# First attention of a gated cross-attention kernel: normalized rows in transposed form, from an input that is laid out transposed as well

## The chip, the core and the metric

The kernel runs on one core of a Trainium2 chip. The core has engines that each take their own instructions in order: TensorE (PE in the profile, with its weight loads as PEld), VectorE (DVE), ScalarE (ACT), GpSimd (POOL) and SyncE (SP), which here issues most of the transfers; sixteen DMA engines move the data. [...] SBUF is the on-chip memory with 128 partitions, PSUM the small memory that PE writes to, DRAM the memory outside. The metric is the device time of one execution in microseconds (us); lower is better.

## What is computed

The reference is a block of two layers on x, two sequences of 2048 rows with 512 features:

```python
x = x + tanh(g_xattn[0]) * xattn0(layernorm(x), ctx)
x = x + tanh(g_ffn[0])   * ffn0(layernorm(x))      # router takes 256 rows of each sequence
x = x + tanh(g_xattn[1]) * xattn1(layernorm(x), ctx)
x = x + tanh(g_ffn[1])   * ffn1(layernorm(x))      # quantized, with a convolution
```

The change is in the first line. There, layernorm takes each row's own mean and variance over the 512 features, without learned factors:

```python
m = mean(x, axis=-1); v = var(x, axis=-1)
xn = (x - m) / sqrt(v + 1e-5)
q = xn @ Wq.T + bq          # 16 heads of 32
att = softmax(q k^T / sqrt(32))       # over the 128 rows of the context
out = (att v) @ Wo.T + bo
```

Keys and values come from the context alone and are made once, at the start. The queries are a product over the features, so PE wants the normalized rows with the features on the partitions: xn transposed.

## The kernel before

The 4096 rows are worked in N = 8 blocks of BLK = 512 rows (TB = 4 tiles of 128 rows; DC = 4 chunks of 128 features). A block has H = 16 units, one for each head. `cross_attention` is a function used for both attentions; in its main loop, U counts units over all blocks, n is the block and u the unit in it, and four units make a group with one query tile qT.

For each unit the loop asks for: scores on PE (once for four heads, into four PSUM tiles sc), the maxima of the scores on DVE (`nmx`, L119), four exponentials on ACT (L122), a reciprocal on DVE (L130) and the division on POOL (L131), all within `probabilities`; two units later, four transposes of the attention weights A on PE (`tp`, L297) and their copy AT by DVE or ACT (L298); after each four units, the product with the values on PE (`po`, L305) and a copy OT by ACT. After a block's last group, the generator `back` is advanced one step for each unit: POOL adds the output bias to the rows of x (L322), PE makes the output projection (`pp`, L328), DVE adds it to x (L339). Then the router of that block runs beside the next block's units: statistics of the new rows (L817), a dot product (L821), a store of x, a scaled row xo on ACT (L845) which is stored, the loads of x for three blocks on, and the ranking by comparisons (`marks` L873, `tie` L917).

What comes before a block's queries is `front(n)`. Before the change it is asked for at unit `ahead` = 10 of the block before: `ln_stats` takes bn_stats and their aggregate on DVE (L99, L100), a small step on DVE (L88) and a power on POOL (L90) for 1/sqrt; `normalize` makes four tiles xn on DVE (L104); `transpose_block` transposes them in sixteen steps on PE into PSUM tiles ptr (L113), and ACT copies those to xnT (L245). `queries` then multiplies xnT with Wq on PE (`pq`, L256), and ACT makes qT with scale and bias (L264). pq, ptr and pp share one PSUM pool, ps_mm, with two buffers. The first block's front stands alone, before the loop.

The order of instructions on each engine isn't the order of the source. A scheduler of the framework builds each engine's order from the requests, moving work forward where it finds an engine free and the buffers allow it; so the row statistics of blocks 1 and 2 stand ahead of the first block's first maxima, already before the change. Once built, the order is fixed, and each engine waits at the head of its own queue. SP's queue is one such order: a transfer that must wait holds those behind it.

At the start, SP loads the context and the key and value weights, four tiles of x, then Wq, biases, Wo, the router's weights, and eight more tiles of x.

Of the kernel before, what the change touches and what calls it, by code (L numbers as in the profile page):

```python
# [10 lines left out]
F32 = mybir.dt.float32  # L11
BF16 = mybir.dt.bfloat16
AF = mybir.ActivationFunctionType
ALU = mybir.AluOpType
# [29 lines left out]
def flamingo_kernel(ctx: ExitStack, tc: tile.TileContext, a: dict, out: bass.AP):  # L44
# [172 lines left out]

    def cross_attention(
        W, act, hold, ps_mm, ps_sc, ps_o, row, xnT_bufs, ahead, rows_of, after_block, beside,
        after_units=lambda: None,  # L220
    ):

# [11 lines left out]
        if bias:  # L234
            nc.vector.tensor_scalar(W.bq, W.bq, scale, None, ALU.mult)

        def front(n):

            tiles, xn, residual = rows_of(n)
            mv, rstd = ln_stats(tiles, L + "ln")  # L240
            for i, t in enumerate(tiles):
                normalize(xn[i], t, mv, rstd, i)
            xnT = act.tile([P, DC, BLK], F32, name="xnT", tag="xnT", bufs=xnT_bufs)
            transpose_block(
                ps_mm, "mm", xn, lambda d, pt: nc.scalar.copy(xnT[:, d, :], pt)  # L245
            )
            return residual, xnT

        def queries(xnT, grp):

# [95 lines left out]


        N = B * NBLK
        residual, xnT = {}, {}
        residual[0], xnT[0] = front(0)  # L350
        next_qT = queries(xnT[0], 0)
        As, AT, OT, out_of = {}, {}, {}, iter(())
        for U in range(N * H + 12):
            n, u = divmod(U, H)
            if n < N:
                grp, t = divmod(u, 4)
                if t == 0:
                    qT = next_qT
                if u % hpc == 0:
                    sc = scores(n // NBLK, qT, u // hpc)  # L360
                As[U] = probabilities(sc[u % hpc])
                if u == ahead and n + 1 < N:
                    residual[n + 1], xnT[n + 1] = front(n + 1)
                if t == 1 and grp < 3:
                    next_qT = queries(xnT[n], grp + 1)
                elif t == 1 and n + 1 < N:
                    next_qT = queries(xnT[n + 1], 0)
            V = U - 2
            if 0 <= V < N * H:
# [386 lines left out]
    with ExitStack() as st:  # L756
# [239 lines left out]

        sel_pools = selected_pools(st)
        W0 = CrossWeights("L0_", D // P, True, gx[0], st, "left")
        nc.scalar.dma_start(out=W0.bk, in_=a["L0_bk"])
        nc.scalar.dma_start(out=W0.bq, in_=a["L0_bq"])  # L1000
        with ExitStack() as st0:
            loads = W0.load_keys(st0, "left")
            next(loads)
            next(loads)
            load_x(0)
            for _ in loads:
                pass
# [22 lines left out]
        for q in selecting:  # L1030
            for _ in q:
# [450 lines left out]
def laid_out(i):  # L1482
# [6 lines left out]
    def col(v, n):  # L1489
# [53 lines left out]
```

## Time and profile before

| | us |
|---|---|
| median of 3 runs | 1741.56 (1740.54 to 1748.13) |
| the profiled execution | 1741.68, of which its span 1740.0 |
| PE busy | 1628.8 (94% of the span) |
| DVE busy | 1240.6 (71%) |
| ACT busy | 1103.3 (63%) |
| POOL busy | 560.1 (32%) |
| first queries of the first attention start | 27.3 |
| first row maxima (L119) start | 33.6 |
| last scores of the first attention start | 497.6 |
| granted clock of TensorE, mean share of full speed | 0.982 |

How to read it: the span is the time between the first and the last instruction of one profiled execution; the rest of its time lies around it. Busy is the sum of an engine's instruction times, in which those that overlap aren't counted twice. A group row of the profile gives the line, the engine, the operation, what it writes and reads with partitions x elements and type, how many there are, then the busy time, the mean of one in ns, and the time for which the engine stood idle just before them, with whom it waited for. A busy share over the whole span is a mean over stages with different limits. The first attention takes about the first 30% of it.

### The profile page before, as it was taken

The page shows a single profiled execution, that of the slowest core. Times are in us where ns is not written, and L with a number is a line of the kernel's source. Part 1 is how long each engine was busy: PE and PEld are TensorE (multiplying, and loading weights), DVE is VectorE, ACT ScalarE, POOL GpSimd, SP SyncE. Part 2 cuts the span into 40 slices and gives each one's busy share as a digit, 9 for nine tenths or more (in the row PEclk, how much of TensorE's full clock was granted, in tenths as well). Part 3 has the DMA queues.
Part 4 walks back from the last instruction along what each step waited for, and adds up shares of the span by engine and source line. Part 5 has one row for each costly group of instructions (what it writes and reads, how often), then busy time and mean ns, then how long its engine had stood idle before and what let it go on. Part 6 is the DMA issues. An engine that isn't in the chain of part 4 may idle for free.

```text
span 1740.0 us, 25223 instructions
## 1 busy us (share of the span) xinstructions
PE 1628.8 (94%) x8076; PEld 856.4 (49%) x8122; DVE 1240.6 (71%) x2576; ACT 1103.3 (63%) x3170; POOL 560.1 (32%) x703
## 2 busy tenths in 40 slices
PE   7999888899999989999999999999999999998988
PEld 4545444455555665755454544445444454444433
DVE  5566777865757543345368889898789889877986
ACT  2876566456553333345267878788787887855575
POOL 2534443442340021033223243343332333343221
PEclk9999999999989999999999999999999999999999
DMA  6011111121005851920011334234133233157294
GB/s 222 7 68 56 37 62 68 61 67 55 25 37 197 274 174 63 300 85 25 19 55 73 122 99 148 92 115 164 73 128 115 88 103 132 78 217 264 100 311 149
DMA packets 116973, 196.99 MB, mean 113 GB/s; under 512 B 13117, under 2 KB 51517, under 8 KB 113129
## 3 DMA queue, kind: packets, MB, share of 16 engines
q1 hardware_dynamic: 110664, 177.54, 29.5%
q0 software_dynamic: 5888, 17.83, 3.2%
q8 instruction: 64, 1.05, 0.2%
q14 instruction: 69, 0.56, 0.1%
q10 hardware_dynamic: 288, 0.00, 0.0%
HBM read 120.89 MB, written 74.45 MB: 112 GB/s over the span
## 4 chain that ended last, share of the span: by engine, by line
PE 48%; DVE 27%; ACT 9%; issue 6%; DMA 6%; POOL 3%; SPq 0%; DVEq 0%; POOLq 0%; ACTq 0%
PE pp L328 12%; PE pq L256 9%; DVE h L1196 4%; PE po L305 4%; PE tp L297 4%; PE sc L279 4%; ACT A L122 3%; PE ph L1179 3%; DVE nmx L119 2%; DVE marks L873 2%; DVE u L1190 2%; DVE AT L298 1%; DMA x<-h_d 1%; DVE L_ln_st L99 1%; DMA h_d<-h 1%
## 5 line engine op out<-in xcount | busy, mean ns | idle before, releaser
L122 ACT ACTIVATE A<-sc,nmx 128x128 f32<-128x128 f32 x1024 | 364.7, 386 | 122.6 <-DVE nmx L119 117.9
L131 POOL TENSOR_TENSOR A<-A,rden 128x512 f32<-128x512 f32 x256 | 280.5, 1098 | 493.9 <-DVE rden L130 402.4
L328 PE MATMUL pp<-L_wo,OT 128*128 128x512 f32 x768 | 360.8, 601 | 5.4 <-DVE x L339 5.4
L256 PE MATMUL pq<-xnT,L_wq 128*128 128x512 f32 x768 | 344.8, 596 | 1.3 <-DVE x L339 1.2
L122 ACT ACTIVATION_READ_ACCUMULATOR A<-sc,nmx 128x1 f32 x1024 | 229.5, 224 | 0.0
L256 PEld LDWEIGHTS pq<-xnT,L_wq 128*128 128x128 f32 x768 | 142.5, 191 | 159.7 <-issue 151.4
L119 DVE TENSOR_REDUCE nmx<-sc 128x4 f32<-128x512 f32 x256 | 168.7, 679 | 67.7 <-PE sc L279 67.6
L328 PEld LDWEIGHTS pp<-L_wo,OT 128*128 128x128 f32 x768 | 134.9, 191 | 148.9 <-issue 130.9
L1196 DVE SCALAR_TENSOR_TENSOR h<-u,cw,h 128x512 f32<-128x512 f32 x256 | 197.2, 803 | 5.8 <-ACT h L1192 5.3
L297 PE MATMUL tp<-ident,A 128*128 128x128 f32 x1024 | 164.8, 285 | 23.5 <-POOL A L131 12.4
L297 PEld LDWEIGHTS tp<-ident,A 128*128 128x128 f32 x1024 | 118.6, 143 | 93.2 <-issue 47.5
L298 DVE COPY AT<-tp 128x512 f32<-128x512 f32 x192 | 130.0, 679 | 38.7 <-PE tp L297 38.1
L279 PEld LDWEIGHTS sc<-L_kT,qT 32*128 32x128 f32 (+1 forms) x2048 | 109.7, 189 | 70.8 <-issue 58.2
L279 PE MATMUL sc<-L_kT,qT 32*128 32x128 f32 (+1 forms) x2048 | 136.2, 291 | 3.7 <-ACT A L122 3.1
L1192 ACT ACTIVATE h<-u,cb,cw 128x512 f32<-128x512 f32 x128 | 99.5, 809 | 62.1 <-DVE u L1190 57.1
L305 PE MATMUL po<-AT,L_v 128*32 128x512 f32 (+1 forms) x512 | 120.1, 655 | 11.5 <-DVE AT L298 11.1
L1409 PE MATMUL po<-w2q,hq 128*128 128x512 bf16 x501 | 117.6, 381 | 9.8 <-ACT hq L1389 6.2
L1179 PE MATMUL ph<-xiT,w1q 128*128 128x512 bf16 x477 | 122.5, 379 | 2.1 <-DVE u L1190 0.2
L1190 DVE TENSOR_TENSOR u<-ph,inv_b 128x512 f32<-128x512 f32 x128 | 85.4, 683 | 31.5 <-PE ph L1179 27.7
L130 DVE RECIPROCAL rden<-den 128x4 f32<-128x4 f32 x256 | 43.6, 170 | 80.3 <-ACT A L122 72.7
L1189 POOL COPY u<-carry 128x2 f32<-128x2 f32 x112 | 44.3, 397 | 150.3 <-DVE h L1196 127.7
L1179 PEld LDWEIGHTS <-w1q 128*128 128x128 bf16 x512 | 49.2, 98 | 79.1 <-issue 35.3
(246 smaller groups left out, 2383.1 us busy)
## 6 DMA issues: line engine op xcount, KB each, us to landing
h_d<-h SPq DMA_DIRECT2D x28, 1024.0 KB, 3.9
x_d<-x SPq DMA_DIRECT2D x64, 256.0 KB, 2.0
hf<-h_d SPq DMA_DIRECT2D x64, 256.0 KB, 3.0
x<-h_d SPq DMA_DIRECT2D x48, 256.0 KB, 5.3
x<-in_x SPq DMA_DIRECT2D x32, 256.0 KB, 3.7
x_d<-xo SPq DMA_DIRECT2D x32, 256.0 KB, 2.0
xf<-x_d SPq DMA_DIRECT2D x32, 256.0 KB, 3.5
x<-x_d SPq DMA_DIRECT2D x32, 256.0 KB, 3.4
```

What stands on the lines that cost most here:

```text
L119: nc.vector.tensor_reduce(nmx, sc, AX.X, ALU.max, negate=True)
L122: nc.scalar.activation(out_tile[:, h, :], sc[:, h, :], AF.Exp, bias=nmx[:, h : h + 1], accum_out=den[:, h : h + 1],)
L131: nc.gpsimd.tensor_tensor(out_tile, out_tile, rden.unsqueeze(2).to_broadcast([P, n, width]), ALU.mult,)
L256: nc.tensor.matmul(pq, W.wq[:, d, ts(e, P)], xnT[:, d, :], start=(d == 0), stop=(d == DC - 1),)
L279: nc.tensor.matmul(sc[h][:, t, :], qT[e % cpg][r, ts(t, P)], W.kT[r, b, e, :], start=True, stop=True,)
L297: nc.tensor.transpose(tp[:, t, :], A[:, t, :], ident)
L298: copy(AT, tp.rearrange("p t n -> p (t n)"))
L305: nc.tensor.matmul(po[h * dh : (h + 1) * dh, :], W.v[:, b, ts(hd, dh)], AT[c * hpc + h], start=True, stop=True,)
L328: nc.tensor.matmul(pp, OT[e][:, ts(i, P)], W.wo[:, e, :], start=(e == 0), stop=(e == nE - 1),)
L1179: nc.tensor.matmul(ph, w1q[:, d, ts(c, P)], xiT[g][:, d, :], start=(d == 0), stop=(d == DC - 1),)
L1190: nc.vector.tensor_tensor(u[:, 2:], ph, inv_b[g], ALU.mult)
L1196: nc.vector.scalar_tensor_tensor(z, u[:, ds(k, BLK)], cw[:, c, k : k + 1], z, ALU.mult, ALU.add)
```

## The change

The input x is given to the kernel a second time, transposed (`xT`, 512 features x 4096 rows). A block's normalized transposed rows are then made in that layout, as xT * (1/sqrt(v+eps)) + (-m/sqrt(v+eps)), where both factors run along the free dimension and must be the same in all 128 partitions. To spread them over the partitions, the first block uses eight PE transposes (`bcast_rows`) into two PSUM tiles; the others write the two 128 x 4 columns to DRAM as rows and load them back, 4 KB into each partition (SP issues all of it). The multiplication is done by DVE in the first block and by POOL in the others, the addition by DVE. The row statistics are still taken from x in its own layout, with DVE and POOL.

The second attention keeps the old way. `front` becomes a generator; one step of it is taken for each unit, from unit 5 of the block before. The first queries of the next block are asked for one unit later in the last group (t == 2 in place of t == 1). A pool xTp with two buffers of 1 MB holds xT; the tiles xn and xnT of this attention are gone, and a tile ln_sp of 4 KB per partition is new. xT of the first block is loaded behind the first four tiles of x.

```diff
     def cross_attention(
         W, act, hold, ps_mm, ps_sc, ps_o, row, xnT_bufs, ahead, rows_of, after_block, beside,
-        after_units=lambda: None,
+        after_units=lambda: None, columns_of=None,
     ):
...
         def front(n):
-            tiles, xn, residual = rows_of(n)
+            if columns_of:
+                residual[n], xnT[n] = yield from columns_of(n)
+                return
+            tiles, xn, residual[n] = rows_of(n)
...
-            return residual, xnT
+            yield
...
-        residual[0], xnT[0] = front(0)
+        for _ in front(0):
+            pass
+        rows_for = iter(())
+        starts = {max(0, n * H + ahead): n + 1 for n in range(N - 1)}
...
-                if u == ahead and n + 1 < N:
-                    residual[n + 1], xnT[n + 1] = front(n + 1)
+                if U in starts:
+                    rows_for = front(starts[U])
+                next(rows_for, None)
                 if t == 1 and grp < 3:
                     next_qT = queries(xnT[n], grp + 1)
-                elif t == 1 and n + 1 < N:
+                elif t == 2 and grp == 3 and n + 1 < N:
                     next_qT = queries(xnT[n + 1], 0)
...
+        xTp = st.enter_context(tc.tile_pool(name="xTp", bufs=2))
+        def load_xT(n):
+            t = xTp.tile([P, DC, BLK], F32, name="xT", tag="xT")
+            nc.sync.dma_start(out=t, in_=row_tiles(a["xT"])[:, :, ts(n, BLK)])
+            return t
...
             load_x(0)
+            xT0 = load_xT(0)
...
-        def stage1_rows(n):
+        def stage1_columns(n):
             tiles = [x[t] for t in range(n * TB, (n + 1) * TB)]
-            xn = [act.tile([P, D], F32, name="xn", tag="xn", bufs=TB) for _ in tiles]
-            return tiles, xn, lambda: tiles
+            xT = xT0 if n == 0 else load_xT(n)
+            st = small.tile([P, TB, 6], F32, name="L0_ln_st", tag="ln_st")
+            mv = small.tile([P, TB, 2], F32, name="L0_ln_mv", tag="ln_mv")
+            for i, t in enumerate(tiles):
+                nc.vector.bn_stats(st[:, i, :], t)
+                nc.vector.bn_aggr(mv[:, i, :], st[:, i, :])
+                if n > 0 and i == 1:
+                    yield
+            rstd = rsqrt(TB, mv[:, :, 1], 1.0, 1e-5, small, "L0_ln_rstd")
+            nmr = row.tile([P, TB], F32, name="nmr0", tag="nmr0")
+            nc.vector.scalar_tensor_tensor(nmr, mv[:, :, 0], -1.0, rstd, ALU.mult, ALU.mult)
+            if n == 0:
+                spread = [ps_mm.tile([P, BLK], F32, name="pb0", tag="mm") for _ in range(2)]
+                for ps, cols in zip(spread, (rstd, nmr)):
+                    bcast_rows(ps, cols, ident)
+            else:
+                sp_d = dramp.tile([2, TB, P], F32, name=f"ln_d{n}")
+                with nc.allow_non_contiguous_dma("columns to rows"):
+                    for k, cols in enumerate((rstd, nmr)):
+                        nc.sync.dma_start(out=sp_d[k].rearrange("j n -> n j"), in_=cols)
+                yield
+                sp = act.tile([P, 2, BLK], F32, name="ln_sp", tag="ln_sp", bufs=1)
+                nc.sync.dma_start(
+                    out=sp.rearrange("p k n -> p (k n)"),
+                    in_=sp_d.rearrange("k j n -> (k j n)").partition_broadcast(P),
+                )
+                spread = [sp[:, k, :] for k in range(2)]
+                for _ in range(3):
+                    yield
+            for d in range(DC):
+                to = xT[:, d, :]
+                scaler = nc.vector if n == 0 else nc.gpsimd
+                scaler.tensor_tensor(to, to, spread[0], ALU.mult)
+                nc.vector.tensor_tensor(to, to, spread[1], ALU.add)
+                if d % 2:
+                    yield
+            return lambda: tiles, xT
...
-            W0, act, act, ps_mm, ps_sc, ps_o, row, 1, 10, stage1_rows,
+            W0, act, act, ps_mm, ps_sc, ps_o, row, 1, 5, None,
             lambda n, tiles: pending.append(router(n, tiles)), beside,
+            columns_of=stage1_columns,
...
         "x": con(np.asarray(i["x"]).reshape(B * S, D)),
+        "xT": con(np.asarray(i["x"]).reshape(B * S, D).T),
```

In the order that is built from this, POOL's queue in the first block holds four divisions, the four multiplications of block 1, eight divisions, the four multiplications of block 2, and then the divisions from the thirteenth on.

More of the change, by code (lines that the diff above doesn't have):

```diff
@@ L235, in cross_attention @@
             nc.vector.tensor_scalar(W.bq, W.bq, scale, None, ALU.mult)
+        residual, xnT = {}, {}
         def front(n):
-            tiles, xn, residual = rows_of(n)
+            if columns_of:
+                residual[n], xnT[n] = yield from columns_of(n)
+                return
+            tiles, xn, residual[n] = rows_of(n)
             mv, rstd = ln_stats(tiles, L + "ln")
@@ L242, in front @@
                 normalize(xn[i], t, mv, rstd, i)
-            xnT = act.tile([P, DC, BLK], F32, name="xnT", tag="xnT", bufs=xnT_bufs)
+            xnT[n] = act.tile([P, DC, BLK], F32, name="xnT", tag="xnT", bufs=xnT_bufs)
             transpose_block(
-                ps_mm, "mm", xn, lambda d, pt: nc.scalar.copy(xnT[:, d, :], pt)
+                ps_mm, "mm", xn, lambda d, pt: nc.scalar.copy(xnT[n][:, d, :], pt)
             )
-            return residual, xnT
+            yield
         def queries(xnT, grp):
@@ L348, in cross_attention @@
         N = B * NBLK
-        residual, xnT = {}, {}
-        residual[0], xnT[0] = front(0)
+        for _ in front(0):
+            pass
+        rows_for = iter(())
+        starts = {max(0, n * H + ahead): n + 1 for n in range(N - 1)}
         next_qT = queries(xnT[0], 0)
```

## The prediction

> **What bounds the kernel now.** I read the 40 slices first, to find which engine is full where; then busy times per stretch of the first attention (about 32 to 525 us); then its groups by shape, for the price of each operation; then the waits and the chain, for what is late.
>
> The slices, engine and tenths busy:
>
> ```profile
> PE   7999888899999989999999999999999999998988
> DVE  5566777865757543345368889898789889877986
> POOL 2534443442340021033223243343332333343221
> ```
>
> A slice is 43.5 us, so the first twelve digits are this attention: TensorE (PE) at eight or nine tenths, VectorE (DVE) at five to eight, GpSimd (POOL) at two to five. By stretch (length, then busy time and instructions of PE, weight loads, DVE, ACT, POOL; clock, DMA share, GB/s):
>
> ```profile
> 33.00:90.00 57.00, 54.20 (x387) 30.09 (x382) 31.11 (x74) 47.15 (x217) 30.05 (x28) 1.00 0.02 6
> 90.00:150.00 60.00, 55.33 (x367) 28.98 (x364) 42.61 (x102) 40.38 (x169) 25.08 (x23) 1.00 0.17 58
> 205.00:265.00 60.00, 52.99 (x360) 27.58 (x353) 45.65 (x102) 37.41 (x154) 25.02 (x22) 1.00 0.16 54
> ```
>
> PE idles 2.8 us in the first stretch and 4.7 and 7.0 in the others; adding the windows between them gives 45.6 us over 33 to 525. So PE bounds, with holes where DVE is late: freed PE time is worth its full length only while nobody else arrives later. The groups that the change touches, in 32 to 525 us:
>
> ```profile
> L113 PE MATMUL ptr<-ident,xn 128*128 128x128 f32 x112 | 17.4, 279 | 0.6 <-ACT qT L264 0.5
> L245 ACT COPY xnT<-ptr 128x512 f32<-128x512 f32 x28 | 16.4, 596 | 15.2 <-PE ptr L113 9.9 <-PE pi L963 5.2
> L104 DVE TENSOR_SCALAR xn<-x,L_ln_mv,L_ln_rstd 128x512 f32<-128x512 f32 x24 | 15.7, 707 | 7.9 <-POOL L_ln_rstd L90 7.8
> L131 POOL TENSOR_TENSOR A<-A,rden 128x512 f32<-128x512 f32 x128 | 141.5, 1110 | 219.6 <-DVE rden L130 184.4 <-DVE m L547 9.6 <-PE pq L256 9.1
> L322 POOL TENSOR_TENSOR x<-x,L_bo 128x512 f32<-128x512 f32 x31 | 40.2, 1298 | 0.0
> ```
>
> The first three are what goes. The fourth is the softmax division that every attention weight passes; what I put on POOL ahead of it delays it. The fifth, two full SBUF inputs, is the nearest row for the new multiplications. Who is late for whom (total us, times, longest):
>
> ```profile
> ACT A L122 <- DVE nmx L119: 75.9, 27, 6.7
> PEld tp L297 <- POOL A L131: 25.8, 22, 2.7
> PE tp L297 <- POOL A L131: 10.6, 12, 2.2
> ```
>
> PE already waits for the division, and the exponentials wait for the row maxima, which stand in DVE's queue. At the start the chain is DVE alone (start, length, what):
>
> ```profile
> 21.36 0.70 DVE L_v L213
> ...
> 22.61 1.00 DVE xn L104 x2
> ...
> 30.03 1.92 DVE xn L104 x4
> ...
> 33.63 0.65 DVE nmx L119
> ```
>
> From 22.15 us to the first maximum at 33.6 DVE works almost without a gap: 11.5 us, nothing to hide in. The transfers nearest to the new ones (size, us to landing):
>
> ```profile
> x_d<-x SPq DMA_DIRECT2D x64, 256.0 KB, 2.0
> xf<-x_d SPq DMA_DIRECT2D x32, 256.0 KB, 3.5
> ```
>
> **The sum, against 1741.7 us** (span 1740.0 and 1.7 around it; the median of the runs is 0.1 lower). I use start-to-start distances: DVE 0.60 for a two-input 128x512 operation or a maximum, 0.80 for bn_stats with its aggregate, 0.48 for xn; PE 0.43 for four transposes; POOL 1.27 and 1.04 for the last two groups.
>
> *Removed.* Per block 16 transposes: 4 x 0.43 = 1.7 us of PE, which sits between other matmuls and so counts. Four ACT copies (4 x 0.6 = 2.4 us) and four xn are off the PE queue.
>
> *xn becomes add, four each.* The Trainium skill (VectorE: DVE Perf Modes, "Why tensor_tensor can't do 2x_2P or 4x") says that a two-tensor operation can't use the doubled f32 mode that a one-tensor operation from SBUF can. At 512 elements and its 0.96 GHz that would be 0.27 against 0.53 us, hence 1.1 us more per block (an estimate from the page). The rows give 0.48 and 0.60: 0.5 us more. And the mean of xn here is 0.71 where its median is 0.54 (one took 1.48 beside a POOL operation), so the old form was not at its best either. I take the rows: 0.5 us, on DVE, small beside what follows.
>
> *Start, +4.2.* The scale and shift rows are made by 8 PE transposes behind the last value matmul (21.3 + 0.9 = 22.3 us). Then DVE's order is: 4 multiplications, 4 additions and both value additions (one was done at 18.8 before): 10 x 0.60 = 6.0; bias gate and weight sum 1.0; bn_stats of the next two blocks 8 x 0.80 = 6.4; two eps steps and two shifts 0.66; waits for POOL's power (1.02 each, the second in full) 1.4. Together 15.5: the first maximum at 37.8, 4.2 later. Before, eight plain xn did this. PE has meanwhile only the second group's queries (3.5 us) and then waits for the first A. The extra 1 MB of xT moves at the 400 GB/s that the start window shows, so what is behind it lands 2.6 us later; Wq, some 4 MB into the queue, landed near 16 us and is needed at 27: hidden.
>
> *Block 0, +2.5 - 2.2 + 2.0.* The built order of POOL is: four divisions, four multiplications for block 1, eight divisions, four multiplications for block 2. The first 5.1 us burst begins when the fourth division ends (41.9 + 4.2 = 46.1) and pushes the fifth from 48.6 to 51.2: +2.5 for PE, whose transposes of A stand next. The transposes of x gone from 54.7 to 58 save 1.7 and a 0.5 hole. The second burst stands ahead of the thirteenth division: 61.2 (end of the twelfth, before) + 5.1 = 66.3 against 63.5; xT of block 2 can only be loaded once block 0's last query is done, about 59, and lands by 64: +2 where PE reaches that transpose.
>
> *Block 1, -1.7*: its transposes go, its multiplications were done already.
>
> *Fronts of blocks 3 to 7, +0.4 each.* Gains: 1.7 of PE. Also the maxima: before, the power (129.0) and four xn (130.05 to 134.1) stand ahead of the group's first maximum at 134.14, while its scores were ready at 130.8. After, only the shift stands there: about 131, 3.1 earlier; but PE idles only 0.95 us in that stretch, so 0.9 is all it can give. Cost: after the shift both columns go to DRAM (0.35 to issue, 2.0 by the store row), SP waits for that landing, issues (0.4) and 512 KB come back spread (3.5 by the load row): 6.3 us, then the first multiplication 1.3. DVE gets to the first addition about 4.8 us after the shift (two reciprocals, a count, a copy of AT, x), so it stands 2.8; the next three come at POOL's 1.27, not 0.60: 2.0 more. Behind it in DVE are the router's statistics, the next evacuation of pp and the next maxima: 4.8 us late. Cover: this is the output projection's stretch, PE is full (pp and pq), and PE needs the next group's first A only some 4.3 us after the earliest possible; but pp shares two PSUM buffers with pq, and the evacuation of pp is late by the whole 4.8. I take 3.0 of PE, between 0 and 7 (no cover, and the divisions behind the burst late as well). -1.7 - 0.9 + 3.0 = +0.4; five times, +2.
>
> The store is not in the trace: 512 elements of 4 bytes. The Trainium skill (DMA: Bandwidth & Descriptors, "Rules for kernel authors") warns that a non-contiguous last dimension becomes one descriptor per element: 32 on each of 16 engines instead of 8. Lower bound: the row's 2.0. Upper: the page's 10.5 ns per packet adds 0.3, and a partial write may double it: 4.3. I take 2.0, which a 128x4 load from DRAM also shows; at 4.3 each front loses up to 2 more. SP: the wait for the store holds the x1 stores behind it some 2 us; nobody reads them within the block. Loads of x for three blocks on already meet their statistics late (DVE waited 5.9 us for them): 0, at most 1 each.
>
> *Traffic:* 8 MB of xT and 3.7 MB of spread rows, at 0.16 of the DMA engines used: hidden. Queries of the next block one unit later: hidden, its qT is needed two units on.
>
> Sum: 4.2 + 2.3 - 1.7 + 2 = +6.8, less 0.5 for ACT's 2.4 us per block where it is full (110 to 116 us): **1748 us**.
>
> **Rivals.** *PE is all that counts:* 8 x 1.7 less 0.9 for the new rows = -12.7, the holes give 0.9 x 6 = -5.4, the new waits are covered, the start costs 4.2: -14, 1728. For it: PE full in all pp stretches. Against: the holes are DVE's and POOL's, and both get more to wait for. *The round trip reaches PE:* without cover a front costs 7, not 3: 5 x 4 = 20 on top, 1768. It decides where PE stands over 4.3 us per front with the addition or the multiplication as releaser. For it: three in-order queues (SP, POOL, DVE) wait for one transfer in turn. Against: the full pp stretches. *The scheduler hides it all but the start:* 1743.
>
> **Numbers.** Within 0.5% (8.7 us) counts as no change. Mixed ledger 0.55 (1740 to 1757; 0.34 no change, 0.21 slower); PE gain 0.18, faster; round trip 0.20, slower; hidden 0.07 (0.05 no change, 0.02 faster). Faster 0.20, no change 0.39, slower 0.41. The range 1729 to 1768 holds the ledger and about half of each outer rival.
>
> **What would show it.** First maximum near 38 us (start); PE idle before the fifth and thirteenth transposes of A (bursts); DVE additions with POOL's multiplication as releaser and some 5 us of DVE idle per front; no ptr in this stage; later stages unchanged in length. A first maximum below 35, or PE idle in 33 to 525 under 45 us, makes me wrong towards faster; over 70, towards slower.

## The result, and the profile after

The changed kernel takes 1849.35 us, the median of 6 runs (1847.03 to 1856.12), beside 1741.05 for the kernel before in 6 runs (1737.67 to 1748.13): a ratio of 1.0623, 95% interval 1.0600 to 1.0646. It is 108 us slower, and the forecast of 1748, with its range up to 1768, was wrong. The profiled execution took 1849.91 us, span 1848.2.

Where the time went is read first from the forty slices of the span. These are the rows of the changed kernel:

```profile
PE   6696868579689998899999999999999999999988
DVE  5555756686666664424536888888798888877976
PEclk8698989888899999999999999999999999999999
```

In the first thirteen slices, the kernel before has PE at 8 and 9 almost throughout; ten of them now hold 5 to 8. DVE fell with it (in the stretch shown below, from 69% busy to 63%). No engine became the bound; all wait. The granted clock of TensorE (PEclk, in tenths) falls in most of the same slices. The first matmul of the feed-forward stage (`acc`) starts at 647.6 us, before at 550.0: 97.6 of the 108 us lie ahead of it. From it to the end of the span it is 1200.6 us, before 1190.0. Most of those 10.6 lie in the second attention: from its first to its last transposes of rows (`ptr` from `xf`) it is 672.2 us, before 662.8. The diff reaches it as well, since the line that asks for the next block's first queries is in the function that both attentions use.

The window from 33 us to that matmul, first of the kernel before, then of the changed kernel (busy time and instructions of PE, PEld, DVE, ACT and POOL, then the clock, the share of the DMA engines and GB/s):

```profile
33.00:550.00 517.00, 470.99 (x2944) 254.90 (x2940) 355.05 (x837) 318.92 (x1303) 211.49 (x191) 0.97 0.15 52
```

```profile
33.00:647.60 614.60, 486.86 (x2842) 255.85 (x2838) 389.51 (x849) 303.26 (x1275) 253.05 (x220) 0.88 0.21 63
```

PE stands still for 614.6 - 486.9 = 127.7 us instead of 46.0, so 82 of the 98 us are waits. The other 16 are busy time, although the transposes of x are gone: with a clock of 0.88 instead of 0.97 the same matmuls last longer. Seven standstills of PE, each over 6 us, make up 70.5 of the 127.7 us; the kernel before has none over 3.2. Two lie in the first block; the others, one in the front of each of the blocks 3 to 7, are these (PE's queue, each with the start, the duration and in brackets the idle time before it and what released it):

```profile
172.36 1.12 PE L303 MATMUL tp<-ident,A 128*128 128x128 f32 x4 [8.40 <-POOL A L131]
263.18 3.78 PE L334 MATMUL pp<-L_wo,OT 128*128 128x512 f32 x4 [13.37 <-DVE x L345]
339.01 3.78 PE L334 MATMUL pp<-L_wo,OT 128*128 128x512 f32 x4 [13.60 <-DVE x L345]
406.67 1.87 PE L952 MATMUL pr<-pick,cnt 128*128 128x4 f32 x8 [6.69 <-DVE cnt L946]
479.63 3.78 PE L519 MATMUL kc<-hT,wqk 128*128 128x256 f32 x8 [13.20 <-DVE qc L524]
```

What the engines wait for, from 32 to 640 us (total, times, longest):

```profile
ACT A L122 <- DVE nmx L119: 154.7, 29, 20.9
DVE xT L1075 <- POOL xT L1074: 72.1, 8, 15.8
POOL xT L1074 <- DMA ln_sp<-ln_d: 65.9, 6, 14.6
...
PE tp L303 <- POOL A L131: 41.3, 14, 9.0
...
PE pp L334 <- DVE x L345: 31.4, 4, 13.6
```

This is one chain, read from the middle: the transfer ln_sp holds POOL, POOL's multiplication holds DVE's addition, and behind these two stand the divisions of A (POOL), the update of x and the row maxima (DVE), for which PE and ACT wait. The waits of ACT on the maxima were 75.9 us before, those of tp on A 10.6.

One front, that of block 3, in SP's queue, then in POOL's, then in DVE's:

```profile
156.50 0.38 SPq L1061 DMA_DIRECT2D ln_d<-nmr  x1
164.73 0.33 SPq L1064 DMA_DIRECT2D ln_sp<-ln_d  x1
```

```profile
154.20 1.01 POOL L90 TENSOR_TENSOR L_ln_rstd<-L_ln_rstd_e,neghalf 128x4 f32<-128x4 f32 x1 [0.46 <-DVE L_ln_rstd_e L88]
...
170.04 1.26 POOL L1074 TENSOR_TENSOR xT<-xT,ln_sp 128x512 f32<-128x512 f32 x1 [11.37 <-DMA ln_sp<-ln_d]
```

```profile
171.34 1.51 DVE L1075 TENSOR_TENSOR xT<-xT,ln_sp 128x512 f32<-128x512 f32 x1 [10.48 <-POOL xT L1074]
```

The second store is issued at 156.5 and the load that needs it at 164.7, since it has to land first; ln_sp comes back 5 us later, 13.5 us after that store was issued. Meanwhile POOL has one division and two bias additions to do (the lines left out) and then stands 11.4 us at the head of its queue. The stores and the load by their issues (size, median us from issue to landing), and SP's own wait for the second store (total, times, longest):

```profile
ln_d<-L_ln_rstd SPq DMA_DIRECT2D x7, 2.0 KB, 8.4
ln_d<-nmr SPq DMA_DIRECT2D x7, 2.0 KB, 8.4
ln_sp<-ln_d SPq DMA_DIRECT2D x7, 512.0 KB, 3.6
```

```profile
SPq L1064 <- DMA ln_d<-nmr: 43.8, 6, 10.4
```

The store of 512 single elements takes 8.4 us in the median (8.2 to 10.8 in the nine whose landing is on record), where the 256 KB store of x takes 2.0 as before. Of the loads only one has its landing on record, and POOL did not wait for that one; from the load's issue to POOL's first multiplication it is 4.1 to 6.1 us in blocks 3 to 7 and 8.7 in block 1.

### The profile page after: what moved, and what is told of

It reads as the page before. It is cut to its first block, busy times and chain, and to the rows that moved or that the text cites. A ratio compares the mean times of both kernels' runs of the same rounds, so it can differ in the third digit from the quotient of the medians.

```text
span 1848.2 us, 25077 instructions
## 1 busy us (share of the span) xinstructions
PE 1652.3 (89%) x8002; PEld 864.1 (47%) x8002; DVE 1279.9 (69%) x2588; ACT 1084.8 (59%) x3138; POOL 602.0 (33%) x731
## 4 chain that ended last, share of the span: by engine, by line
PE 50%; DVE 27%; DMA 9%; ACT 6%; POOL 4%; issue 3%; SPq 0%; DVEq 0%; POOLq 0%; ACTq 0%
PE pp L334 11%; PE pq L262 11%; DVE h L1251 5%; PE po L311 4%; PE sc L285 4%; PE tp L303 4%; PE ph L1234 3%; DVE nmx L119 3%; DVE marks L882 2%; DMA ln_d<-nmr 2%; PE pu L668 2%; PE pw L668 2%; PE acc L653 2%; ACT A L122 2%; DMA hf<-h_d 2%
## 5 line engine op out<-in xcount | busy, mean ns | idle before, releaser
L334 PE MATMUL pp<-L_wo,OT 128*128 128x512 f32 x768 | 371.5, 617 | 31.9 <-DVE x L345 31.8
L262 PE MATMUL pq<-xnT,L_wq 128*128 128x512 f32 x512 | 228.7, 597 | 2.0 <-DVE x L345 2.0
L334 PEld LDWEIGHTS pp<-L_wo,OT 128*128 128x128 f32 x768 | 139.1, 196 | 185.0 <-issue 140.8
L1251 DVE SCALAR_TENSOR_TENSOR h<-u,cw,h 128x512 f32<-128x512 f32 x256 | 202.8, 825 | 3.3 <-ACT h L1247 3.1
L303 PEld LDWEIGHTS tp<-ident,A 128*128 128x128 f32 x1024 | 122.0, 147 | 127.7 <-POOL A L131 64.5
L285 PEld LDWEIGHTS sc<-L_kT,qT 32*128 32x128 f32 (+1 forms) x2048 | 118.5, 194 | 73.4 <-issue 57.4
L285 PE MATMUL sc<-L_kT,qT 32*128 32x128 f32 (+1 forms) x2048 | 146.4, 296 | 3.4 <-ACT A L122 3.3
L262 PEld LDWEIGHTS pq<-xnT,L_wq 128*128 128x128 f32 x512 | 95.1, 190 | 112.1 <-issue 101.9
L262 PE MATMUL pq<-xT,L_wq 128*128 128x512 f32 x256 | 128.0, 640 | 6.6 <-issue 4.6
```

Of the source, the lines that this page charges most:

```text
L262: nc.tensor.matmul(pq, W.wq[:, d, ts(e, P)], xnT[:, d, :], start=(d == 0), stop=(d == DC - 1),)
L285: nc.tensor.matmul(sc[h][:, t, :], qT[e % cpg][r, ts(t, P)], W.kT[r, b, e, :], start=True, stop=True,)
L303: nc.tensor.transpose(tp[:, t, :], A[:, t, :], ident)
L334: nc.tensor.matmul(pp, OT[e][:, ts(i, P)], W.wo[:, e, :], start=(e == 0), stop=(e == nE - 1),)
L1251: nc.vector.scalar_tensor_tensor(z, u[:, ds(k, BLK)], cw[:, c, k : k + 1], z, ALU.mult, ALU.add)
```

## The experiments

All runs stand beside runs of the kernel before on the same chip (medians 1738.8 to 1744.2 us from set to set); a ratio is to those. T1 is that the way through DRAM with its in-order queues costs the time; T2 that additions on DVE and multiplications on POOL slow each other when they run side by side; T3 that the moved requests cost it; T4 that TensorE's clock, which falls after a standstill, makes every wait longer. T5 came in the middle.

### The way of the rows, taken apart (T1, T2)

**e1_pe_spread**: no DRAM; PE spreads the columns, ACT copies them.

```diff
-                sp_d = dramp.tile([2, TB, P], F32, name=f"ln_d{n}")
...
+                ps2 = [ps_mm.tile([P, BLK], F32, name="pb0", tag="mm") for _ in range(2)]
+                for ps, cols in zip(ps2, (rstd, nmr)):
+                    bcast_rows(ps, cols, ident)
                 yield
                 sp = act.tile([P, 2, BLK], F32, name="ln_sp", tag="ln_sp", bufs=1)
-                nc.sync.dma_start(
...
+                for k in range(2):
+                    nc.scalar.copy(sp[:, k, :], ps2[k])
```

> Every block's scale and shift rows are spread by eight PE transposes and two ACT copies; the store to DRAM and the load back are gone, the rest is as in the changed kernel. Theory 1 (three in-order queues stand for the trip through DRAM): nearly all of the 108 us goes, 1735 to 1775 us, and POOL waits for no transfer. Theory 2 (additions on DVE and multiplications on POOL slow each other down, 1.73 us an addition): at most a third goes, over 1810. Theory 3 (the new order: fronts of two blocks in the first one, from unit 5, queries a unit later): over 1815.

1779.29 us, ratio 1.0233 (1.0203 to 1.0263), just above the range of the first theory: 70 of the 108 us go with the trip through DRAM. The waits of POOL on the load of ln_sp are gone, DVE's on POOL fall to 7.4 us, PE's on A to 20.1. Forty remain.

**e2_rows_store**: PE transposes the two columns first, so that the store writes 8 runs of 512 bytes; the way through DRAM stays.

```diff
+                for k, cols in enumerate((rstd, nmr)):
+                    nc.tensor.transpose(pr[0:TB, ts(k, P)], cols, ident)
...
-                        nc.sync.dma_start(out=sp_d[k].rearrange("j n -> n j"), in_=cols)
+                nc.sync.dma_start(out=sp_d.rearrange("k j n -> j k n"), in_=rows[0:TB])
```

> The two columns are first turned into rows by two PE transposes and one ACT copy, and stored as eight runs of 512 bytes in place of 1024 elements of 4 bytes; still through DRAM. Theory 1 with the store's elements as cause: the store lands in about 2.2 us, not 8.2, and with 6 us less per front and a faster PE clock the time is 1770 to 1805. If the trip as such is the cause, whatever its store: over 1820.

1795.09 us, 1.0324 (1.0294 to 1.0354). SP's queue in the front of block 3, and SP's own wait for the store:

```profile
159.14 0.27 SPq L1066 DMA_DIRECT2D ln_d<-rows  x1
160.43 0.32 SPq L1069 DMA_DIRECT2D ln_sp<-ln_d  x1
```

```profile
SPq L1069 <- DMA ln_d<-rows: 7.0, 7, 1.2
```

The load can be issued 1.3 us after this store, where 8.2 us pass in the changed kernel. The waits of POOL on ln_sp fall from 65.9 to 27.9 us, and half of the loss is gone. The built order changed too, but not in blocks 4 to 6, where again 3, 3 and 2 operations of POOL stand between rstd and the first multiplication: there the waits fall from 11.1, 13.0 and 7.6 us to 3.4, 3.8 and 0. So the landing of the store matters. It doesn't follow that a slow store must cost: e13 below keeps it and loses as little.

**e3_stale_rows**: the load reads the rows of the block before, so it needn't wait for this block's store (blocks 2 to 7 then get wrong rows).

```diff
-                    in_=sp_d.rearrange("k j n -> (k j n)").partition_broadcast(P),
+                    in_=stored.get(n - 1, sp_d).rearrange("k j n -> (k j n)").partition_broadcast(P),
```

> Blocks 2 to 7 are normalized with the rows of the block before, so that the load back needn't wait for the store just made; stores, loads, multiplications and additions are all still there (the output differs). Theory 1: without that wait 1745 to 1785. If the small elements cost by filling the DMA engines, or by what they hold up: over 1820. Theory 2: over 1810.

1805.51 us, 1.0384 (1.0353 to 1.0414). This lies in none of the expected ranges. The wait of POOL on ln_sp is down to 8.3 us and one case, and still 67 us are lost, with PE waiting 54.2 us on A. The scheduler also built another order here: the load stands right behind the store that it reads (8.1 us after it in block 4), and in blocks 4 to 7 the multiplications stand 6 to 13 operations of POOL behind the rstd that they use, where the changed kernel has 1 to 3. So this run doesn't isolate the wait; it shows that much is lost without it. That the multiplications on POOL are to blame is suggested by the waits on A; e17 below tests it in another order.

**e4_dve_mult**: all multiplications on DVE, the way through DRAM as it is.

```diff
-                scaler = nc.vector if n == 0 else nc.gpsimd
+                scaler = nc.vector
```

> All multiplications by DVE, none by POOL; the trip through DRAM is kept. Theory 2: additions fall from 1.73 to 0.7 us and the time to 1800 or less. Theory 1: the wait for the rows is the same, now on DVE alone, and POOL's divisions are free of it; 1815 to 1850.

1822.05 us, 1.0479 (1.0448 to 1.0509): 27 us better. Multiplications and additions last 0.685 us each, and DVE itself now waits 58.1 us for ln_sp. One queue less stands in the wait; the wait stays.

**e5_before_stores**: the kernel before, with the two stores per block that nobody reads.

```diff
                 normalize(xn[i], t, mv, rstd, i)
+            if bias and n > 0:
+                sp_d = dramp.tile([2, TB, P], F32, name=f"ln_d{n}")
...
+                        nc.sync.dma_start(out=sp_d[k].rearrange("j n -> n j"), in_=cols)
```

> The kernel before, with two stores added in each of blocks 1 to 7: one statistic per row, [128 x 4] of single 4-byte elements, from SBUF to DRAM, that nobody reads (14 stores, nothing of the computation is left out). T1 (what the change lost through its store is the wait for it, not the traffic): the stores land in 8 us or more here too, and the time stays within 5 us of before, 1736 to 1746. Rival (the scattered 4-byte packets hold up other transfers on the same queue and engines): 1760 or more, with waits on loads grown.

1741.84 us, 1.0011 (0.9985 to 1.0037). The traffic of the scattered stores costs nothing that can be measured. Their landing isn't on record here, since nothing waits for it, so the expected 8 us stand untested in this kernel.

**e7_pe_dve**: e1 with all multiplications on DVE (the one-word edit of e4).

> The changed kernel with the scale and shift rows of blocks 1 to 7 spread by TensorE and two ScalarE copies instead of DRAM (as in the run e1_pe_spread, 1779), and with all multiplications on VectorE instead of GpSimd. Against e1: T2 (additions and multiplications that run side by side on VectorE and GpSimd slow each other, and GpSimd's queue holds up the transposes of A) expects both to fall to about 0.65 us an operation, no wait of TensorE on GpSimd's A in the fronts, and 1755 to 1768. Rival (VectorE is the fuller engine in stage 1, 28 more operations of 0.65 us there cost what they gain): 1774 to 1790, with TensorE waiting on VectorE instead.

1776.91 us, 1.0211 (1.0146 to 1.0276), within the uncertainty of e1. The additions did become faster, which the next lines show, first of e1, then of e7 (duration in ns, minimum, median and maximum):

```profile
L1071 POOL TENSOR_TENSOR xT<-xT,ln_sp x28: 1262/1706/2182, 59.8 to 430.3; 128x512 f32<-128x512 f32 x28
L1072 DVE TENSOR_TENSOR xT<-xT,ln_sp x28: 676/1128/1756, 61.1 to 432.6; 128x512 f32<-128x512 f32 x28
```

```profile
L1071 DVE TENSOR_TENSOR xT<-xT,ln_sp x28: 655/678/1521, 57.1 to 424.4; 128x512 f32<-128x512 f32 x28
L1072 DVE TENSOR_TENSOR xT<-xT,ln_sp x28: 637/677/1528, 59.1 to 425.7; 128x512 f32<-128x512 f32 x28
```

Side by side the two operations do slow each other, but between these two runs that isn't worth time: T2 is true as an observation and falls as a cause. (In another built order the same edit is worth 20 us, e17.) PE waits on A as much as in e1 (21.2 us).

### The times of request (T3)

**e8_old_times**: e7 with the front at unit 10 and the next block's first queries at t 1, as before the change.

```diff
-                elif t == 2 and grp == 3 and n + 1 < N:
+                elif t == 1 and grp == 3 and n + 1 < N:
...
-                for _ in range(3):
-                    yield
...
-            W0, act, act, ps_mm, ps_sc, ps_o, row, 1, 5, None,
+            W0, act, act, ps_mm, ps_sc, ps_o, row, 1, 10, None,
```

> As e7_pe_dve, but the front of the next block starts where it does in the kernel before (10 units into a block instead of 5, without the three steps of waiting, the next block's first queries asked for in the unit before). T3 (the moved request times cost time by themselves, in stage 1 and by a different order in the later stages): 8 to 20 us less than e7, and the later stages within 4 us of before. Rival (the times of request cost nothing; the remainder is in the start, in VectorE's work and in TensorE's clock): within 5 us of e7 in either direction.

1752.55 us, 1.0074 (1.0039 to 1.0109): 24 us back, 13.7 of it ahead of the first `acc`, 7.2 in the second attention (665.6 us by the measure above, in e7 672.8).

**e12_first_queries**: e7 with the first line of that diff alone.

> As e7_pe_dve (1777), with one word changed: the next block's first queries are asked for one unit earlier, as in the kernel before; the front still starts at unit 5. If the later request of those queries is what e8_old_times took back, e12 lies near e8, 1750 to 1760. If it is the place of the front (its statistics and additions in VectorE's queue among other units), e12 stays at 1768 to 1780.

1755.11 us, 1.0059 (1.0042 to 1.0077). Nearly all of it is the queries' place, 16.2 us ahead of `acc` and 11.3 in the second attention of the profiled runs; the front's place makes no difference that can be measured.

**e18_before_late**: the kernel before with its queries at t 2.

> The kernel before with the next block's first queries asked for one unit later, at t 2 instead of t 1, and nothing else. If the place of the queries costs by itself, because TensorE and the row maxima behind it are short of scores at each block's first unit: 1755 to 1766. Rival (it costs only where xT is late too, or the scheduler moves the queries forward anyway): within 5 us of before.

1754.74 us, 1.0072 (1.0042 to 1.0102): 12.5 us, just below what was expected. The later request costs by itself, but not where I looked for it. The first attention is only 1.2 us longer. The transposes of the second one, in the kernel before and in e18 (first and last start):

```profile
L113 PE MATMUL ptr<-ident,xf x128: 270/273/332, 744.7 to 1407.5; 128*128 128x128 f32 x128
```

```profile
L113 PE MATMUL ptr<-ident,xf x128: 271/273/332, 747.7 to 1419.3; 128*128 128x128 f32 x128
```

There it is 671.6 us instead of 662.8: 8.8 of the 12.5. All ten kernels with the line at t 2 have 670.2 to 673.1 there; those with t 1 have 660.2 to 667.2, but for e11 and e15 with 672.3 and 670.5. The order of TensorE's work in this stage is one and the same in all traces with t 1, these two included, and another one in all with t 2. In e11 and e15 the traces record half clock for 20.5 and 17.5 us of the stage, in the others with t 1 for 0 to 13.7 us; why, no run shows.

**e9_first_old**: e8 with block 0 normalized in rows and transposed.

```diff
+            if n == 0:
+                mv, rstd = ln_stats(tiles, "L0_ln")
...
+                transpose_block(ps_mm, "mm", xn, lambda d, pt: nc.scalar.copy(xT[:, d, :], pt))
+                return lambda: tiles, xT
-            xT = xT0 if n == 0 else load_xT(n)
+            xT = load_xT(n)
```

> As e8_old_times, but block 0 is normalized in rows and transposed as in the kernel before, so that the start is the old one and the transposed input of block 0 is not loaded. The start alone (first row maxima of the changed kernel 3.5 us later than before) makes e9 3 to 6 us faster than e8. If TensorE's time saved by the 112 transposes counts once waits and contention are gone, e9 comes out at 1730 to 1745, at or below before; if the clock granted to TensorE falls in the first 100 us here too, it stays 10 us or more above before.

1748.77 us, 1.0036 (1.0008 to 1.0064): 3.8 us less than e8, as much as the start was predicted to cost, though the intervals of the two overlap. With no DRAM, no POOL multiplications and the old requests, the transposed form is still not faster than before. PE's spreading products take 8 of the 16 transposes' places. From 33 us up to `acc` PE stands idle about as long as before (44.4 against 46.0 us), but it is busy for 476.0 us instead of 471.0, at a mean clock of 0.95 instead of 0.97.

### The order that is built (T5)

**e10_early_store**: the changed kernel with statistics and stores asked for two units earlier.

```diff
-        starts = {max(0, n * H + ahead): n + 1 for n in range(N - 1)}
+        starts = {n * H + ahead - (2 if columns_of and n else 0): n + 1 for n in range(N - 1)}
...
-                yield
+                for _ in range(3 if n > 1 else 1):
+                    yield
```

> The changed kernel with one thing moved: in blocks 2 to 7 the statistics and the two stores are asked for two units earlier, about 8 us at some 4 us a unit; the load of ln_sp, the GpSimd multiplications and everything after them stay in their units (block 1 is as it was). T1 (time is lost while SP's, GpSimd's and VectorE's queues wait in turn for the 8 us landing of the store) expects the waits of GpSimd on ln_sp to fall from 66 us to under 25 and most of what the TensorE spread of e1 gained, 1780 to 1805. Rival (the earlier request finds rows of x that have not landed, or the load is asked for late whatever the store does): within 15 us of the changed kernel, 1835 to 1860, with VectorE waiting on x.

1854.34 us, 1.0626 (1.0509 to 1.0743): nothing gained, and not for the reason given for the rival. The trace of block 3's front shows it (POOL's queue of e10):

```profile
157.33 1.01 POOL L90 TENSOR_TENSOR L_ln_rstd<-L_ln_rstd_e,neghalf 128x4 f32<-128x4 f32 x1 [0.46 <-DVE L_ln_rstd_e L88]
...
173.39 1.26 POOL L1075 TENSOR_TENSOR xT<-xT,ln_sp 128x512 f32<-128x512 f32 x1 [11.59 <-DMA ln_sp<-ln_d]
```

From rstd to the first multiplication it is 16 us, as in the changed kernel (154.20 to 170.04). The request moved, the place in the built order didn't: in most blocks again 3 operations of POOL stand between the two.

**e11_early_dve**: e9, but with the rows of blocks 1 to 7 through DRAM and the front's place as in e10: from unit 5, the stores two units earlier.

> As e9_first_old (block 0 by rows and transposes, multiplications on VectorE, the next block's first queries one unit earlier than in the changed kernel), but the scale and shift rows of blocks 1 to 7 go through DRAM as in the changed kernel, the stores asked for two units earlier in blocks 2 to 7. If a round trip through DRAM costs nothing once it is asked for early and no GpSimd work hangs on it, e11 loses 8 of TensorE's spreading products and two ScalarE copies per front against e9 and comes out at 1738 to 1752. Rival (landing times vary so much, 3.6 to 10.8 us, that some fronts still wait): 1760 or more, with VectorE waiting on ln_sp.

1802.43 us, 1.0329 (1.0198 to 1.0460), with DVE waiting 40.7 us on ln_sp: the same wait, without POOL.

So T5: the scheduler seems to count on the rows sooner than they land, and puts what needs them too close behind. Where the order can be pinned, the same trip should cost little.

**e13_pinned**: the changed kernel, with each multiplication and addition held behind what its engine was asked for before.

```diff
-                scaler.tensor_tensor(to, to, spread[0], ALU.mult)
-                nc.vector.tensor_tensor(to, to, spread[1], ALU.add)
+                pin = tc.keep_in_program_order if n > 0 else lambda ins: ins
+                pin(scaler.tensor_tensor(to, to, spread[0], ALU.mult))
+                pin(nc.vector.tensor_tensor(to, to, spread[1], ALU.add))
```

> The changed kernel with one thing added: every multiplication and addition of blocks 1 to 7 is held behind all that its engine was asked for before it, so the scheduler cannot move it forward. In GpSimd's built order 6 to 13 divisions of A now stand between the power that makes rstd and the first multiplication, where 1 to 5 stood. T5 (the built order, which takes the round trip for shorter than it is, makes the wait): each division is a half unit or more of other work, so most of the wait of GpSimd on ln_sp (66 us) goes, and the time falls to 1775 to 1810. Rival (the trip holds up SP's and VectorE's queues whatever the place): 1835 or more.

1793.91 us, 1.0285 (1.0234 to 1.0336): 55 us back, by the order alone. POOL's wait on ln_sp falls from 65.9 to 1.2 us, although the stores land as late as before (9.0 us in the median). The same front in SP's and in POOL's queue of e13:

```profile
148.66 0.38 SPq L1061 DMA_DIRECT2D ln_d<-nmr  x1
156.95 0.33 SPq L1064 DMA_DIRECT2D ln_sp<-ln_d  x1
```

```profile
167.09 1.04 POOL L131 TENSOR_TENSOR A<-A,rden 128x512 f32<-128x512 f32 x1 [7.49 <-DVE rden L130]
169.31 2.48 POOL L131 TENSOR_TENSOR A<-A,rden 128x512 f32<-128x512 f32 x2
171.76 2.49 POOL L1075 TENSOR_TENSOR xT<-xT,ln_sp 128x512 f32<-128x512 f32 x2
```

The load is issued 8.3 us after the store, as ever, but from the power to the multiplication at 171.76 POOL now does eight divisions, and then finds its rows there. In blocks 3 to 7 it does 4 to 10 of them in that place, where the changed kernel has 0 to 2 (not 1 to 5, as the expectation has it).

**e14_early_pinned**: e10 with the pins of e13.

> e10_early_store (1854: statistics and stores two units earlier) with the multiplications and additions held in their place as in e13: 10 to 13 divisions between. T5: the wait of GpSimd on ln_sp falls below 10 us and the time comes to that of e1_pe_spread or a little under, 1765 to 1785, since what is left is the start, the later first queries and TensorE's clock. Rival as for e13: 1835 or more. If the two differ by less than 5 us, the place alone was enough.

1791.57 us, 1.0272 (1.0222 to 1.0321), higher than expected, and the same as e13. The place was enough; more lead gives nothing.

**e15_early_dve_pinned**: e11 with the pins.

> e11_early_dve (1802) with the multiplications and additions, here all on VectorE, held in their place. T5: VectorE's wait on ln_sp (41 us) falls below 8 us, and the time comes to that of e9_first_old (1749) or under it by what TensorE saves without the spreading products, 1738 to 1752. Rival (28 more operations and the held order delay the row maxima in VectorE's queue): 1765 or more, with ScalarE waiting on nmx.

1760.66 us, 1.0102 (1.0060 to 1.0143): 42 us better than e11, the wait on ln_sp gone, yet 12 above e9, between the two ranges that were expected. PE stands 4.07 us before tp on A once in each of four blocks, which it doesn't in e9.

### What remains in e13

**e16_pinned_queries**: e13 with the queries at t 1. **e17_pinned_queries_dve**: e16 with all multiplications on DVE. Both edits are shown above.

> e13_pinned (1794) with the next block's first queries asked for one unit earlier, as in the kernel before. If their place costs what it did between e7 and e12, 1770 to 1780. Rival (GpSimd's multiplications decide when xT is ready, so earlier queries only wait in TensorE's queue): 1790 or more, with TensorE's weight loads waiting on xT.

> e16 with all multiplications on VectorE; the round trip through DRAM, the start of the changed kernel and its place of the front stay. If GpSimd's multiplications ahead of the divisions of A are the second cause, TensorE's wait on A falls from 43 us to under 20 and the time to 1755 to 1765, the start's 4 us and TensorE's clock being the rest to before. Rival (VectorE's 28 more operations cost as much): within 5 us of e16.

1789.86 us, 1.0273 (1.0206 to 1.0339), and 1769.69 us, 1.0157 (1.0086 to 1.0228). The queries' place gives 4 us here, no more than the uncertainty, and nothing ahead of `acc` (which starts at 592.5 us, in e13 at 591.7): as the rival said, earlier queries don't help. Its reason is not shown: PE's weight loads wait only 6.5 us on xT (4.6 in e13). The multiplications on POOL are worth 20 us, which is more than the uncertainty, and PE's waits on A fall from 29.1 to 19.1 us; the time stays above the 1755 to 1765 that were expected.

## Why the prediction was wrong, point by point

**The start, +4.2: right.** The first maximum starts at 37.10 us (37.8 predicted, 33.6 before), and e9 gains 3.8 on e8, about as little as the runs can tell.

**The fronts, +0.4 each: this step failed.** I reckoned 2.0 us for the store's landing and 3.5 for the load, 6.3 us for the trip with its issues, so DVE 2.8 us short and PE 3.0. The store took 8.4 us in the median, outside its bounds of 2.0 to 4.3, and from the load's issue to the multiplication it was 4.1 to 6.1 us. In block 3 the trip took 13.5 us. The row that I took for the store was that of 256 KB in long runs. The upper bound came from a price per packet in the Trainium skill (DMA: Bandwidth & Descriptors), which stands there for loads issued from GpSimd, in "Measured (HBM→SBUF, 128 partitions, SWDGE, issued from GpSimd)". The warning against single elements, in "Rules for kernel authors", pointed the right way; the price explains 0.3 of the 6 us. I took the lower bound although the warning spoke against it. With the late rows DVE stood 10.5 us in block 3, and PE 6.7 to 13.6 us in each front of the blocks 3 to 7.

**The cover** was the second part of that step. I read from the built order that few operations stood between, and took PE's queue as cover for the rest. The stand of POOL and DVE stopped A, the maxima and the evacuation of pp together, so nothing covered. The shares by the runs: 55 us of the 108 go by moving the multiplications and additions in the queues alone (e13 against the changed kernel), 70 by leaving out the trip (e1).

**The rival "round trip reaches PE" (1768) had the mechanism**, three in-order queues that wait for one transfer in turn, and nearly its test: PE standing over 4.3 us per front. It stood 6.7 to 13.6, though not behind the multiplication or addition itself: what released it was the work behind these (A, x, the router's counts and qc). Its price was too small, because it capped PE's loss at 7 us a front from the same 6.3 us trip.

**The multiplications on POOL.** The place was right: PE idle before the fifth and thirteenth transposes of A. It was 9.0 and 6.2 us instead of 2.5 and 2.0, since the first burst waits for late rows, too. For the later blocks the sum had 2.0 us of DVE a front and no lost divisions; even without the wait they are worth 20 us (e16 to e17).

**"Queries one unit later: hidden" was wrong**, and I asked it of one attention only. It is 12.5 us in the kernel before (e18), 8.8 of them in the second attention; 22 between e7 and e12; 4 in e16, within the uncertainty. In the changed kernel its share in the first attention lies beneath the other losses, so these shares can't simply be added.

**xn to addition, 0.5 us a block.** The additions took 1.73 us in the median in the changed kernel, beside POOL's multiplications, but alone 0.68. The size was wrong, the conclusion that it is small held: e7 gains only 2 us on e1.

**PE's gain, -1.7 a block**, wasn't seen in any run. In e15, with the first block alone still transposed, PE is busy 469.2 us up to the first `acc`, before 471.0; its clock there is 0.94 instead of 0.97.

**"Later stages unchanged in length" was wrong by 10.6 us**, 9.4 of them in the second attention, by that same line: e18, which changes nothing else, has the same order of TensorE's work there and 8.8 us more.

**The test that I named** was right: PE idle in stage 1 above 70 us means slower. It was 127.7. The fall of the clock, which lengthens what PE still does by some 16 us net, was in neither the sum nor a rival.

What stays open: the 27 us by which e17 lies above before. The start is some 4 of it. e15 suggests that the rest is the hold on the order (PE's short waits on A in each block) and TensorE's clock (from 33 us up to `acc` 0.93 in e17, before 0.97); no run separates these two.

## What to carry to other kernels

A round trip through DRAM costs little by its traffic and much by its place: look in the built order at what each engine does between the producer and the first consumer, and price the gap by the landing time of the very transfer, not of a large one. Where a scheduler builds the order, asking earlier may move the consumer along with the producer; hold the consumer in place instead. And when a front is moved, test the moved requests alone on the kernel before: here one line of that kind cost 12 us by itself, most of it in another stage that shares the function.

## What the runs showed of the hardware

**A store of single 4-byte elements lands late.** 512 elements from a [128 x 4] tile took 8.4 us (8.2 to 10.8) in the changed kernel and 256 KB of x 2.0. SP waited at most 1.2 us for the landing when both columns went out as 8 runs of 512 bytes (e2). With nobody waiting, the scattered stores cost nothing that can be measured (e5). It isn't the moving of data that takes so long: between 160 and 164 us, while the store of 156.5 is on its way, the DMA engines are busy for a share of 0.00 (first line below, the number before the last). What does take the time, no run shows.

**TensorE's granted clock falls while it stands, and stays down after.** Windows of 4 us around the standstill of block 3's front in the changed kernel (columns as above; the clock is the number after POOL, the share of the DMA engines the next):

```profile
160.00:164.00 4.00, 3.95 (x13) 1.64 (x11) 0.86 (x3) 4.00 (x21) 0.00 (x0) 1.00 0.00 0
164.00:168.00 4.00, 0.00 (x0) 0.00 (x0) 0.00 (x0) 0.51 (x4) 0.00 (x0) 0.83 0.39 24
168.00:172.00 4.00, 0.00 (x0) 0.00 (x0) 0.66 (x1) 0.00 (x0) 1.96 (x2) 0.50 0.46 173
172.00:176.00 4.00, 3.64 (x8) 1.93 (x8) 1.62 (x2) 0.00 (x0) 4.00 (x4) 0.50 0.02 4
```

The four matmuls of pp at 173.27 last 3.62 us instead of 1.88 at full clock. At all six standstills of over 6 us before 410 us the clock falls to between 0.50 and 0.59 in such windows, and the kernel before has no standstill over 4 us in this stage. It falls in a few other windows too, beside short gaps. From 33 us up to `acc` the trace records half clock for 143 of the 614.6 us, before for 31 of 517. The Trainium skill (TensorE: Matmul & The Clock Gate, "Part 1: The HAM clock gate") puts both the fall and the return at about 3.4 us of idle or busy time. The halving agrees; the return took longer here, from 5 us of work (from 339.0 to 344.1 us) to 10 (from 61.0 to 71, with PE busy throughout). The rule belonged into the sum: a standstill of 8 us is followed by matmuls at half speed in each of these fronts. So a wait seems to be paid for twice (T4), which the trace shows at every long wait; no run set the clock alone, so its own share isn't measured.
